# Own matmuls one step ahead, in the other half of the same PSUM banks, and a border that runs over 64 steps

## The chip, the cores and the metric

The kernel runs on one core of a Trainium2 chip. The metric is the time of one execution in microseconds of device time. The engines are named as in the profile: PE is TensorE's matmul stream and PEld its weight loads, DVE is VectorE, ACT is ScalarE, POOL is GpSimd, and SP issues most of the DMAs.

## The reference

The input `x` is 4 images of 64 channels, 256 x 256, in fp32. Two layers follow, each a group norm, a mixing step and a residual sum. Layer 0 is not touched by the change. Layer 1 is a GRU that runs over the columns of the image:

```python
def step(prev_col, cur_col):
    nb = jnp.concatenate([pad, prev_col, pad], axis=1)
    x = jnp.concatenate([nb[:, :-2], nb[:, 1:-1], nb[:, 2:]], axis=-1)
    new = _gru_cell(x.reshape(B * H, 3 * Cf), cur_col.reshape(B * H, Cf), ...)
    ...
# the cell: gi = x @ w_ih.T + b_ih, gh = h @ w_hh.T + b_hh, then
r = sigmoid(i_r + h_r);  z = sigmoid(i_z + h_z);  n = tanh(i_n + r * h_n)
return (1.0 - z) * n + z * h
```

The roles are unusual. The "input" of the cell is the result of the column before, at the rows h-1, h and h+1 (three taps). Its "hidden state" is the normalized column itself. So the products with `w_hh` depend on the input alone and can be made at any time, while those with `w_ih` need the column just finished. There are 255 steps, one after another.

## The kernel before

**Layout of layer 1.** A column of all four images is a tile of 128 partitions (two images x 64 channels) x 2 slots x 256 rows. Every product is done as four 64 x 64 quarters of TensorE's array (`quarters`, line 810): the row half of the array picks one of the two slots of a PSUM tile, the column half one of the two halves of the partitions. A PSUM tile of a gate is `[P, 2, 512]` in fp32, so it has two banks, one for each slot. Four such tiles, `hr`, `hn`, `hz` and `ni`, fill all eight banks. Before the change only 256 of the 512 columns of a bank are used.

**A step** (`column`, line 822) makes for column w:

- own matmuls of three gates (line 826): r into `pshr`, n into `pshn`, z into `pshz`, each of four quarters with 256 rows and the weights `wh`, from the normalized column `xn` and a copy `xt` with swapped halves;
- taps: three gates of three taps, of four quarters each, with the weights `wi` from the state `st` of the column before. The taps of r and z add to the own matmuls in `pshr` and `pshz`; those of n go to `psni` by themselves.

The rows are cut in two parts, [0, at) and [at, 256). `parts` (line 799) moves the border up by one row in each step, so that part 0 of a step, which needs one row more to each side, reads part 0 of the step before alone. After `SKEW` steps the border jumps back; a step where it has jumped is called a wrap (`wraps`, line 849), and there part 0 needs both parts of the step before. With `SKEW = 32` part 0 has 144 rows at a wrap and 113 at the end, part 1 has 112 to 143.

**The order on TensorE** is the program's order; a wrapper keeps every engine's instructions in it. In a usual step it is: own r; taps r of part 0; own n; own z; taps n and z of part 0; taps r, n and z of part 1. At a wrap the three own groups come first. The profile counts each fp32 matmul as two instructions, so four quarters are 8 and a group of taps is 24.

**Behind the taps** `state` (line 864) does, for each part: on ACT `g` = sigmoid of `pshr`, a normalize for a later column (`xn<-raw`), `z` = sigmoid of `pshz`, then tanh; on DVE a scalar_tensor_tensor from `pshn` and `g` (`n<-pshn,bias_sb,g`), the sum with `psni`, a scalar_tensor_tensor `g<-z,xn`, a product `n<-n,z` and the difference that writes the state `st`. POOL copies `xt`, adds the state to the raw column and clears the edges of the state tiles.

Waits between engines are put in by the framework that builds the program, tile by tile, from what each instruction reads and writes.

Of the kernel before, what the change touches and what calls it, by code (L numbers as in the profile page):

```python
# [9 lines left out]
F32 = mybir.dt.float32  # L10
# [5 lines left out]
B, C, W, H = 4, 64, 256, 256  # L16
HID = 6 * C
E = 2 * C
P = 128
# [143 lines left out]
def tile_conv_then_gru(  # L163
# [47 lines left out]
    with tc.tile_pool(name="xa", bufs=5) as xa, tc.tile_pool(name="sta", bufs=1) as sta, tc.tile_pool(  # L211
        name="bps", bufs=1, space=PSUM
# [9 lines left out]
        banks = bps.tile([P, 8, 512], F32, tag="b", name="psb")  # L222
# [7 lines left out]
        for i in range(32):  # L230
            kind, s = i // 16, i % 16
            c0, num = 2 * P * kind, 2 * P - P * kind
            ps = banks[0:HALO, 4 * (i % 2) : 4 * (i % 2) + 4, 0:num]
            for k in range(4):
# [6 lines left out]
                    stop=True,  # L241
# [34 lines left out]
    with layer0 as s:  # L276
# [19 lines left out]
        def normalize(n, jq):  # L296

            t, b, at = xq[n, jq], n // 8, n % 8
            flat = t.rearrange("p j k -> p (j k)")
            shift, rstd = sc0[:, b, 0:1], sc0[:, b, 1:2]  # L300
            if jq == 3:
                nc.vector.tensor_scalar(flat, flat, rstd, shift, ALU.mult, ALU.add)
            else:
                nc.scalar.activation(flat, flat, AF.Identity, bias=shift, scale=rstd)
            grid = t.rearrange("p j (r c) -> p j r c", c=10)
            if jq % 2 == 0:
                nc.gpsimd.memset(grid[:, 0, :, 0:1], 0.0)
            else:
                nc.gpsimd.memset(grid[:, 15, :, 9:10], 0.0)
            if at == 0 and jq < 2:  # L310
                nc.gpsimd.memset(grid[0:C, :, 0, :], 0.0)
            if at == 7 and jq >= 2:
                nc.gpsimd.memset(grid[C:P, :, 9, :], 0.0)
# [427 lines left out]
    WB = 8  # L741
    with ExitStack() as s:
# [3 lines left out]
        ps_g = s.enter_context(tc.tile_pool(name="ps_g", bufs=1, space=PSUM))  # L746
        raws, xns, xts, stcols = {}, {}, {}, {}
# [11 lines left out]
        def load_column(w):  # L759
            raws[w] = rawp.tile([P, 2, H], F32, tag="raw", name=f"raw_{w}")  # L760
            for of, to in column_parts(x1, w):
                nc.sync.dma_start(to, of)
# [5 lines left out]
        def empty_states(n):  # L768
            stcols[n] = st = colp.tile([P, 2, WB, H + 2], F32, tag="st", name=f"st_{n}")
            nc.gpsimd.memset(st[:, :, :, 0:1], 0.0)  # L770
            nc.gpsimd.memset(st[:, :, :, H + 1 : H + 2], 0.0)
# [19 lines left out]
        def add(w):  # L791
            nc.gpsimd.tensor_tensor(raws[w], raws[w], stcols[w // WB][:, :, w % WB, 1 : H + 1], ALU.add)
            for to, of in column_parts(out, w):
                nc.sync.dma_start(to, of)

        QUARTERS = ((0, 0), (0, 1), (1, 0), (1, 1))
        SKEW = 32

        def parts(w):


            at = H // 2 + SKEW // 2 - (w - 1) % SKEW
            return (0, at), (at, H)

        MAX = H // 2 + SKEW // 2

        def bank_pair(gate, w):
            return ps_g.tile([P, 2, 512], F32, tag=gate, name=f"ps{gate}_{w}")

        def quarters(ps, weights, rhs, start, stop, skip=False):  # L810
            for r, c in QUARTERS:
                nc.tensor.matmul(
                    ps[c * C : (c + 1) * C, r],
                    lhsT=weights[r * C : (r + 1) * C],
                    rhs=rhs(r, c),
                    start=start,
                    stop=stop,
                    tile_position=(r * C, c * C),
                    skip_group_check=skip,
                )  # L820

        def column(w):

            i, xn, xt, st = w % WB, xns[w // WB], xts[w // WB], stcols[(w - 1) // WB]

            def own(gate, bank, stop):

                ps = bank_pair(bank, w)[:, :, 0:H]
                quarters(
                    ps,  # L830
                    wh[:, gate, :],
                    lambda r, c: (xn[:, c] if r == c else xt)[r * C : (r + 1) * C, i, :],
                    True,
                    stop,
                )
                return ps

            def taps(ps, gate, h0, h1, start, skip=False):
                for t in range(3):
                    quarters(  # L840
                        ps,
                        wi[:, 3 * gate + t, :],
                        lambda r, c: st[r * C : (r + 1) * C, c, (w - 1) % WB, h0 + t : h1 + t],
                        start and t == 0,
                        t == 2,
                        skip,
                    )

            wraps = (w - 1) % SKEW == 0
            pr = own(0, "hr", False)  # L850
            pn = own(2, "hn", True) if wraps else None
            pz = own(1, "hz", False) if wraps else None
            for part in range(2):
                h0, h1 = parts(w)[part]
                pi = bank_pair("ni", f"{w}_{part}")[:, :, 0 : h1 - h0]
                taps(pr[:, :, h0:h1], 0, h0, h1, False, part == 1)
                if pz is None:
                    pn = own(2, "hn", True)
                    pz = own(1, "hz", False)
                taps(pi, 2, h0, h1, True)  # L860
                taps(pz[:, :, h0:h1], 1, h0, h1, False, part == 1)
                state(w, part, pn[:, :, h0:h1], pr[:, :, h0:h1], pi, pz[:, :, h0:h1])

        def state(w, part, pn, pr, pi, pz):
            h0, h1 = parts(w)[part]
            i, num = w % WB, h1 - h0
            xn, st = xns[w // WB], stcols[w // WB]
            g = gk.tile([P, 2, MAX], F32, tag=f"g{part}", name=f"g_{w}_{part}")[:, :, 0:num]
            n = gk.tile([P, 2, MAX], F32, tag=f"n{part}", name=f"n_{w}_{part}")[:, :, 0:num]
            z = gk.tile([P, 2, MAX], F32, tag=f"z{part}", name=f"z_{w}_{part}")[:, :, 0:num]  # L870
            nc.scalar.activation(g, pr, AF.Sigmoid, bias=b_rz[:, 0:1], scale=1.0)
            for more in range(ahead(w - 1), ahead(w)):
                normalize(more, part)
            nc.vector.scalar_tensor_tensor(n, pn, bias_sb[:, 5:6], g, ALU.add, ALU.mult)
            nc.vector.tensor_tensor(n, pi, n, ALU.add)

            nc.scalar.activation(z, pz, AF.Sigmoid, bias=b_rz[:, 1:2], scale=-1.0)
            nc.scalar.activation(n, n, AF.Tanh, bias=bias_sb[:, 2:3], scale=1.0)
            nc.vector.scalar_tensor_tensor(g, z, -1.0, xn[:, :, i, h0:h1], ALU.add, ALU.mult)
            nc.vector.tensor_tensor(n, n, z, ALU.mult)  # L880
            nc.vector.tensor_tensor(st[:, :, i, 1 + h0 : 1 + h1], n, g, ALU.subtract)

        def ahead(w):

            return min(2 * w + 4, w + WB + 1, W)
# [5 lines left out]
                normalize(w, slot)  # L891
        empty_states(0)
        nc.vector.tensor_copy(stcols[0][:, :, 0, 1 : H + 1], xns[0][:, :, 0])
        for w in range(W):
            if w % WB == 0 and w + WB < W:
                empty_states(w // WB + 1)
            if w:
                column(w)
            add(w)
            if w + 2 * WB < W:  # L900
                load_column(w + 2 * WB)
# [60 lines left out]
```

## Time and profile before

| | |
|---|---|
| runs of the kernel before | 5144.2, 5144.63, 5165.15 us; median 5144.63 us |
| the profiled execution | 5172.3 us, its span 5170.4 us |
| layer 0 and what lies between, by the first own matmul of layer 1 | the first 3806 us of the span |
| layer 1, first own matmul to last tap | 1356.5 us for 255 steps |
| most usual step of layer 1 | 5.23 us |
| granted TensorE clock of the profiled execution | 0.988 |

The profile is one execution on the chip, taken by the hardware profiler. Its rows give the busy time of an engine, or groups of instructions, or single instructions in order of time. All of this kernel's instructions are recorded by one helper, so every row has the same line number, L157, and the names of the tiles tell the rows apart: `pshr<-xn,wh` is an own matmul of r, `pshr<-st,wi` a tap of r. Matmuls overlap, and a row of 24 taps starts before the ones ahead of it have ended; lengths of groups on TensorE are therefore taken from the start of one to the start of the next.

### The profile page before, as it was taken

How to read it: one execution, taken by the hardware profiler on the slowest of the kernel's cores; microseconds unless marked ns; L12 is line 12 of the kernel's file. 1: busy time of each engine (PE TensorE's matmuls, PEld its weight loads, DVE VectorE, ACT ScalarE, POOL GpSimd, SP SyncE). 2: the span in 40 equal slices, each digit the busy share in tenths (PEclk: the TensorE clock that was granted, in tenths of full speed). 3: DMA queues.
4: the chain of work that ended last, by engine and by line, in shares of the span. 5: the costliest groups of instructions: out<-in, count | busy, mean ns of one | idle time of the engine just before them, and what ended most of it. 6: DMA issues, size and time to landing. Idle time of an engine off the chain costs nothing.

```text
span 5170.4 us, 276110 instructions
## 1 busy us (share of the span) xinstructions
PE 4885.9 (94%) x127092; PEld 4252.5 (82%) x127092; DVE 4033.3 (78%) x7000; ACT 3323.6 (64%) x4253; POOL 1732.9 (34%) x1723
## 2 busy tenths in 40 slices
PE   3999999999999999999999999999969999999999
PEld 2878788888888788888787888888859999999998
DVE  4778788888788777887787878777867777777777
ACT  3666666666666566666566667666656666666665
POOL 0233333333333233333333324323243333333333
PEclk9999999999999999999999999999989999999999
DMA  7566676666667666566666656556543333333332
GB/s 257 152 163 174 166 187 174 174 164 171 170 176 185 166 169 173 167 173 174 169 180 173 168 140 162 152 160 169 147 111 105 104 102 103 103 106 102 104 102 73
DMA packets 421176, 784.57 MB, mean 152 GB/s; under 512 B 32604, under 2 KB 295552, under 8 KB 417632
## 3 DMA queue, kind: packets, MB, share of 16 engines
q1 hardware_dynamic: 366464, 533.76, 38.3%
q0 software_dynamic: 53264, 232.55, 15.4%
q8 instruction: 997, 16.33, 1.4%
q14 instruction: 163, 1.34, 0.1%
q10 hardware_dynamic: 288, 0.58, 0.1%
HBM read 622.72 MB, written 144.05 MB: 148 GB/s over the span
## 4 chain that ended last, share of the span: by engine, by line
PE 83%; issue 5%; ACT 4%; DMA 4%; DVE 3%; POOL 1%; ACTq 0%; POOLq 0%; SPq 0%; DVEq 0%
PE psring L157 58%; PE pshr L157 8%; PE pshz L157 8%; PE psni L157 6%; DMA t<-t_all 2%; PE pshn L157 2%; DVE wk L157 1%; ACT v L157 1%; ACT z L157 1%; ACT xq L157 1%; DVE z L157 1%; DVE bn L157 0%; DMA seen<-in_x 0%; DMA bt<-in_taps 0%; DMA wk<-in_sums 0%
## 5 line engine op out<-in xcount | busy, mean ns | idle before, releaser
L157 PEld LDWEIGHTS psring<-h,t 100*32 100x32 f32 x49152 | 1392.0, 120 | 252.0 <-issue 199.8
L157 PE MATMUL psring<-h,t 100*32 100x128 f32 x49152 | 1475.4, 258 | 97.7 <-issue 61.8
L157 PEld LDWEIGHTS psring<-w_sb,xq 64*100 64x100 f32 x24576 | 1371.8, 164 | 128.1 <-issue 93.7
L157 PE MATMUL psring<-w_sb,xq 64*100 64x128 f32 x24576 | 1429.9, 273 | 38.1 <-issue 24.1
L157 ACT COPY h<-psring 100x1024 f32<-100x1024 f32 (+2 forms) x1371 | 1235.2, 988 | 336.7 <-PE psring L157 335.5
L157 DVE TENSOR_TENSOR wk<-psring,wk 128x1024 f32<-128x1024 f32 (+1 forms) x768 | 759.2, 1036 | 469.3 <-PE psring L157 333.6
L157 POOL TENSOR_TENSOR v<-v,z 128x2048 f32<-128x2048 f32 x128 | 582.9, 4558 | 672.9 <-DVE wk L157 611.5
L157 DVE TENSOR_TENSOR z<-z,moments 128x2048 f32<-128x2048 f32 x256 | 577.9, 2278 | 2.3
L157 POOL TENSOR_TENSOR wk<-wk 128x1024 f32<-128x1024 f32 x128 | 303.4, 2370 | 614.0 <-DVE wk L157 561.9
L157 POOL TENSOR_TENSOR raw<-raw,st 128x512 f32<-128x512 f32 x256 | 303.6, 1186 | 539.0 <-DVE st L157 412.4
L157 ACT COPY z<-psring 128x2048 f32<-128x2048 f32 x128 | 239.0, 1867 | 351.1 <-PE psring L157 261.7
L157 ACT ACTIVATE z<-pshz,b_rz 128x288 f32<-128x288 f32 (+7 forms) x510 | 242.5, 476 | 338.5 <-PE pshz L157 333.0
L157 PE MATMUL pshr<-st,wi 64*64 64x144 f32 (+7 forms) x12240 | 450.7, 270 | 7.4 <-DVE st L157 6.6
L157 PE MATMUL psni<-st,wi 64*64 64x144 f32 (+7 forms) x12240 | 445.7, 269 | 0.2
L157 PE MATMUL pshz<-st,wi 64*64 64x144 f32 (+7 forms) x12240 | 445.5, 269 | 0.0
L157 DVE COPY h<-psring 100x1024 f32<-100x1024 f32 x229 | 276.9, 1211 | 208.8 <-PE psring L157 208.6
L157 PEld LDWEIGHTS pshr<-st,wi 64*64 64x64 f32 x12240 | 379.1, 133 | 50.2 <-DVE st L157 38.0
L157 ACT COPY wk<-psring 128x1024 f32<-128x1024 f32 x256 | 259.7, 1014 | 249.8 <-PE psring L157 221.0
L157 DVE BATCH_NORM_STATS2 lnst<-z 128x6 f32<-128x128 f32 x2048 | 416.7, 280 | 0.0
L157 ACT COPY v<-psring 128x2048 f32<-128x2048 f32 (+1 forms) x160 | 243.4, 1521 | 257.8 <-PE psring L157 257.5
L157 PEld LDWEIGHTS psni<-st,wi 64*64 64x64 f32 x12240 | 391.0, 133 | 21.5 <-issue 0.4
L157 PE MATMUL psring<-wk,g_sb 32*64 32x512 f32 x6144 | 383.0, 604 | 7.8 <-issue 3.8
(96 smaller groups left out, 6298.0 us busy)
## 6 DMA issues: line engine op xcount, KB each, us to landing
t<-t_all SPq DMA_DIRECT2D x768, 400.0 KB
xq<-in_xh POOLq DMA_DIRECT2D x128, 800.0 KB, 6.4
wk<-in_x SPq DMA_DIRECT2D x256, 256.0 KB
x<-wk POOLq DMA_DIRECT2D x256, 256.0 KB, 5.4
seen<-in_x POOLq DMA_DIRECT2D x96, 512.0 KB, 7.7
raw<-x SPq DMA_DIRECT2D x128, 256.0 KB
raw<-x SPq DMA_DIRECT2D x256, 128.0 KB
out<-raw SPq DMA_DIRECT2D x128, 256.0 KB
```

The source lines that it names most:

```text
L157: return self.tc.keep_in_program_order(got(*args, **kwargs))
```

## The change

`SKEW` goes from 32 to 64, so part 0 has 160 rows at a wrap and 97 at the end, and part 1 has 96 to 159. The four PSUM tiles are made once instead of once per use. Even and odd steps use columns 0 to 255 and 256 to 511 of the same banks, and for `ni` part 0 and part 1 do. The own matmuls of step w + 1 are all issued behind the last taps of step w, in the order r, n, z. At a wrap the own n of the step after it is issued ahead of the taps, and left out of the place behind them.

```diff
-        SKEW = 32
+        SKEW = 64
...
-        def bank_pair(gate, w):
-            return ps_g.tile([P, 2, 512], F32, tag=gate, name=f"ps{gate}_{w}")
+        banks = {g: ps_g.tile([P, 2, 512], F32, tag=g, name=f"ps{g}") for g in ("hr", "hn", "hz", "ni")}
+
+        def half_banks(gate, odd):
+            return banks[gate][:, :, 256 * odd : 256 * odd + 256]
...
-        def column(w):
-
-            i, xn, xt, st = w % WB, xns[w // WB], xts[w // WB], stcols[(w - 1) // WB]
-
-            def own(gate, bank, stop):
-
-                ps = bank_pair(bank, w)[:, :, 0:H]
+        owns = {}
+
+        def own(w, gates=(0, 2, 1)):
+            i, xn, xt = w % WB, xns[w // WB], xts[w // WB]
+            for gate in gates:
+                owns[w, gate] = half_banks(("hr", "hz", "hn")[gate], w % 2)
                 quarters(
-                    ps,
+                    owns[w, gate],
                     wh[:, gate, :],
                     lambda r, c: (xn[:, c] if r == c else xt)[r * C : (r + 1) * C, i, :],
                     True,
-                    stop,
+                    gate == 2,
                 )
-                return ps
+
+        def column(w):
+
+            st = stcols[(w - 1) // WB]
...
-            wraps = (w - 1) % SKEW == 0
-            pr = own(0, "hr", False)
-            pn = own(2, "hn", True) if wraps else None
-            pz = own(1, "hz", False) if wraps else None
+            if (w - 1) % SKEW == 0 and w + 1 < W:
+                own(w + 1, (2,))
+            pr, pz, pn = (owns.pop((w, gate)) for gate in range(3))
             for part in range(2):
                 h0, h1 = parts(w)[part]
-                pi = bank_pair("ni", f"{w}_{part}")[:, :, 0 : h1 - h0]
+                pi = half_banks("ni", part)[:, :, 0 : h1 - h0]
                 taps(pr[:, :, h0:h1], 0, h0, h1, False, part == 1)
-                if pz is None:
-                    pn = own(2, "hn", True)
-                    pz = own(1, "hz", False)
                 taps(pi, 2, h0, h1, True)
                 taps(pz[:, :, h0:h1], 1, h0, h1, False, part == 1)
                 state(w, part, pn[:, :, h0:h1], pr[:, :, h0:h1], pi, pz[:, :, h0:h1])
+            if w + 1 < W:
+                own(w + 1, (0, 1) if (w + 1, 2) in owns else (0, 2, 1))
...
         nc.vector.tensor_copy(stcols[0][:, :, 0, 1 : H + 1], xns[0][:, :, 0])
+        own(1)
         for w in range(W):
```

## The prediction

> **What bounds the kernel now.** I read the page first, then the windows by stage, the list of waits inside layer 1, and last the timeline of single steps. The page says which engine fills the span:
>
> ```profile
> PE 4885.9 (94%) x127092; PEld 4252.5 (82%) x127092; DVE 4033.3 (78%) x7000; ACT 3323.6 (64%) x4253; POOL 1732.9 (34%) x1723
> ```
>
> That is a mean over both layers. The windows (length, busy time of PE, PEld, DVE, ACT and POOL, granted clock, DMA share, GB/s) show the middle of layer 1:
>
> ```profile
> 4000.00:4500.00 500.00, 497.04 (x15828) 468.05 (x15824) 390.38 (x942) 335.54 (x755) 191.77 (x307) 1.00 0.36 103
> ```
>
> TensorE is idle for 3 us in 500, at full clock. From one first own matmul to the next I read a step as 5.23 us in most of the 255 cases, the same for any border: an own group takes 0.432 us, a group of taps 0.0155 us + 0.005 us a row (0.725 for 142 rows, 0.586 for 114), so 3 x 0.432 + 6 x 0.0155 + 3 x 256 x 0.005 = 5.23. 255 such steps are 1334 us, and the layer takes 1356.5. No order of the same matmuls can win more than those 23 us, 0.45%. The waits inside the layer (us in total, times, longest) say where some of it lies:
>
> ```profile
> PEld pshr L157 <- DVE st L157: 38.0, 108, 1.5
> PE pshr L157 <- DVE st L157: 6.6, 7, 1.0
> ...
> PEld pshz L157 <- ACT z L157: 1.5, 6, 0.3
> PEld pshn L157 <- DVE n L157: 1.4, 6, 0.4
> ```
>
> The first two are taps that wait for the state, mostly covered by matmuls still running. The last two are small, but are what the change multiplies: an own n that waits for VectorE's read of `pshn`, an own z that waits for ACT's read of `pshz`. Before, that can show only at wraps, where own n and z stand straight behind own r. The timeline at a wrap, behind a part 1 of 143 rows:
>
> ```profile
> 4488.14 0.51 DVE L157 SCALAR_TENSOR_TENSOR n<-pshn,bias_sb,g 128x286 f32<-128x286 f32 x1
> 4488.34 0.38 PE L157 MATMUL pshr<-xn,wh 64*64 64x256 f32 x1
> ...
> 4488.77 0.38 PE L157 MATMUL pshn<-xn,wh 64*64 64x256 f32 x1
> ...
> 4490.36 0.46 DVE L157 TENSOR_TENSOR st<-n,g 128x286 f32<-128x286 f32 x1
> 4490.87 0.97 PE L157 MATMUL pshr<-st,wi 64*64 64x144 f32 x24 [0.89 <-DVE st L157]
> ```
>
> The read of `pshn` ends at 4488.65, before own n is due at 4488.77: no wait. The taps then wait 0.89 us for part 1 of the state and start 0.05 after it ends. The next step, part 1 of 112 rows:
>
> ```profile
> 4494.85 0.38 PE L157 MATMUL pshr<-xn,wh 64*64 64x256 f32 x1
> ...
> 4494.88 0.46 DVE L157 TENSOR_TENSOR st<-n,g 128x288 f32<-128x288 f32 x1
> ...
> 4495.16 0.45 ACT L157 ACTIVATE z<-pshz,b_rz 128x224 f32<-128x224 f32 x1
> ...
> 4495.26 0.44 DVE L157 SCALAR_TENSOR_TENSOR n<-pshn,bias_sb,g 128x224 f32<-128x224 f32 x1
> 4495.40 0.96 PE L157 MATMUL pshr<-st,wi 64*64 64x143 f32 x24
> ...
> 4496.18 0.38 PE L157 MATMUL pshn<-xn,wh 64*64 64x256 f32 x1
> ```
>
> Now the read of `pshn` ends at 4495.70, 0.85 us after own r starts. Before it costs nothing, since the taps of r stand between. Behind own r, own n would be due at 4495.28.
>
> **What is added: own n waits for the same bank.** The halves would remove the wait if waits went by columns. The built order of the changed kernel says they don't. Followed to the instruction that each count belongs to, own n of step w + 1 waits for VectorE's `n<-pshn,bias_sb,g` of step w, part 1; own z for ACT's z of step w, part 1; own r for ACT's g. All three read the other half of the bank. Taps n of part 1 still wait for the sum with `psni` of part 0, so the halves of `ni` free nothing.
>
> The trace can't show whether columns apart matter, as before reuses the same ones. The Trainium skill, "PSUM — Partial Sum Buffer", section "PSUM bank collisions raise a hardware error", gives the rule that speaks against this change: guard PSUM by bank and quadrant, not by address, because two engines in one bank collide at any column. Guarded by address the sum would be about -12 us (the removed part below, without the own z term), by bank it is the one below.
>
> So each own n starts at the later of T + 0.432 (T is the start of own r) and the end of VectorE's read + 0.055, the release measured where taps wait for the state. I read that end over all steps, as medians by the rows of part 1: 0.849 us behind T at 112, 0.726 at 118, 0.606 over 127 to 129, 0.41 to 0.50 at 136 to 140, 0.320 at 143. It falls because part 1's taps cover the chain that precedes the read: z of part 0 on ACT, tanh, product, state, then this read; VectorE keeps its order, so the read stands behind part 0's state. By blocks of a new cycle of 64 steps, the wait being lag + 0.055 - 0.432:
>
> - 96 to 111 rows: not in the trace. The slope from 112 to 118, 0.0205 a row, carries on (a row less takes 0.015 of cover and lengthens four operations): mean lag 1.023, wait 0.646, x 16 = 10.3 us. If the lag stayed flat at 0.849 it would be 7.6.
> - 112 to 127: mean lag 0.728, wait 0.351, x 16 = 5.6.
> - 128 to 143: what is over zero sums to 1.9.
> - 144 to 159: none.
>
> Own z is due at T + 0.863; ACT's z of part 1 ends 0.75 (112 rows) to 0.864 (143) behind T. Only where own n does not wait does it show: 0.03 rising to 0.11, 1.35 us over the last 20 steps. A cycle costs 17.9 + 1.35 = 19.2, and 255 steps are four cycles: **+77 us**. What queues behind own n is all of TensorE; own n and own z hold back every tap of the next step.
>
> **What is removed.** Taps r of part 0 wait after each border jump: steps 1 to 7 of a cycle are longer by 0.165, 0.14, 0.12, 0.09, 0.075, 0.05, 0.03, together 0.67, x 8 = 5.4 us. After the change own n's wait ends later than that state does, so this goes whole. Wraps: 7 steps of 6.47 instead of 5.23, 8.7 us. After it 3 remain; with four own groups ahead (1.73 us) and part 1's state about 2.5 behind T, each waits some 0.75, 2.3 us. On the step after a wrap own n is done early, and own z waits 0.38 in place of own n's 0.8: -1.6 over four. Together -5.4 - 8.7 + 2.3 - 1.6 = **-13.4**.
>
> **Edits with no price.** The wider border leaves TensorE's sum of taps at 5.23 (rows sum to 256). Own matmuls one step early need `xn` and `xt` of w + 1, at the same place of the stream as own r before. SP's and POOL's queues are not reordered. Own n of step 2 ahead of the first taps moves 0.9 us of work, not adds it. Taps n and z of part 0 follow r at once now, so `g` and the sum with `psni` have 1.31 us less 0.3 of cover, and needed 1.8 behind taps r against a tanh that waits for z anyway until 2.1: 0.3 spare.
>
> **Sum.** 77 - 13.4 = +64 us. The profiled execution would go from 5172.3 to about 5236; it stands 27.7 above the median, and I carry the difference over: 5144.63 + 64 = 5209. Bounds of the main term: a flat lag under 112 rows takes off 4 x 2.7 = 11, and the lower ones of the scattered lags 5 to 8 more; the upper ones, 0.1 us on some 40 waiting steps, add 17. So +45 to +81, 5190 to 5226.
>
> A second page speaks of such idle time. "TensorE: Matmul & The Clock Gate", "A second HAM failure mode: psum-queue depth-cycling", tells of frequent small idles that make the clock fall. The trace has gaps of 0.89 us at clock 1.00, and I set nothing; by the page, half clock in the 45 or so waiting steps of a cycle would be, as an estimate from their 5.2 us, 900 us.
>
> **Rivals.**
>
> - *The halves work, no own group waits.* Then only the removed part counts: -5.4 - 8.7 + 2.3 = -12 us, 5133, not slower (within 0.5%). It decides if own n starts 0.432 behind own r at 96 rows. For it: nothing else in the trace holds TensorE. Against: the waits in the built order. 5%.
> - *The spare 0.3 us above is not there*, since VectorE is 78% busy, and its sum with `psni` comes late in every step. Then late steps wait too, by about 0.2 us: 255 x 0.2 = 51 more, 5260. For it: VectorE's chain already ends close to TensorE's turn. Against: it ends part 1's state 2.5 us behind T, before taps r of part 0 are read. 10%.
> - *The lags shrink*, because part 0's own chain starts at the same time but with nothing of the step before left on VectorE: below half of the term, about 5165 or less. 3%.
>
> **How the numbers follow.** My forecast has 82%: 5209, range 5190 to 5226. For 8 in 10 I widen for the second rival and for the spread of the runs before (5165.15 lies 20 above their median): 5186 to 5240. About 0.5%, 26 us, is what a measurement of this kernel can tell from no change. Faster by more needs over 23 us won, the whole idle time: 1%. Same: the first and third rivals, 7%. Slower: 92%.
>
> **What would show it.** Right: in the waits of layer 1, `pshn` on DVE n rises from 1.4 us and 6 times to the largest wait of TensorE, some 60 to 80 us over 160 to 180 steps; steps start a cycle near 6.0 us, fall by 0.02 each, and reach 5.25 to 5.30 from about 140 rows; waits of `pshr` taps on DVE st all but vanish outside 3 wraps. Wrong: own n starts 0.43 behind own r at 96 rows; steps at 150 rows over 5.35; or a granted clock under 0.95 in this layer.

## The result and the profile after

| | before | after |
|---|---|---|
| median of six runs each | 5145.49 us (5133.86 to 5165.15) | 5200.45 us (5196.04 to 5208.04) |
| ratio, after to before | | 1.0108, 95% interval 1.0089 to 1.0128, so 46 to 66 us |
| profiled execution, span | 5172.3, 5170.4 us | 5200.1, 5198.2 us |
| first own matmul of layer 1 | 3806.0 us into the span | 3768.5 us |
| layer 1, first own matmul to last tap | 1356.5 us | 1421.9 us, +65.3 |

The change is slower by 55 us, where 64 was forecast. The two profiled executions differ by 28 us only: the one before reached layer 1 some 37 us later, over code that the change does not touch. So layer 1 is compared by itself, in all that follows.

The page after has the same engine on top, busy for 25 us more with the same number of instructions:

```profile
PE 4910.6 (94%) x127092; PEld 4200.5 (81%) x127092; DVE 4053.6 (78%) x7000; ACT 3343.7 (64%) x4253; POOL 1732.8 (33%) x1723
```

In the windows (columns as before) TensorE's idle time in 500 us of layer 1 has grown from 3 us to 10 and 16, at an unchanged clock of 1.00:

```profile
4000.00:4500.00 500.00, 490.06 (x15230) 430.54 (x15223) 385.89 (x907) 330.30 (x725) 185.56 (x297) 1.00 0.35 99
4500.00:5000.00 500.00, 484.08 (x14941) 422.61 (x14934) 374.13 (x889) 322.94 (x711) 179.45 (x289) 1.00 0.34 98
```

The busy time hides part of the loss, since ends of matmuls are modelled. The waits of layer 1 after the change (us, times, longest) name it:

```profile
PEld pshn L157 <- DVE n L157: 106.1, 195, 0.9
...
PE pshn L157 <- DVE n L157: 27.7, 85, 0.5
PEld pshz L157 <- ACT z L157: 24.7, 89, 0.6
...
PEld pshr L157 <- DVE st L157: 3.0, 3, 1.0
...
PE pshr L157 <- DVE st L157: 1.7, 3, 0.6
```

Own n waiting for VectorE has gone from 1.4 us and 6 times to the largest wait of TensorE. Taps waiting for the state have gone from 108 times to the 3 wraps. A weight load's wait (PEld) overlaps the matmuls still running, and a row of PE counts only from the modelled end of the matmuls before it; the time lost to own n lies between the two. A step early in a cycle, behind a part 1 of 97 rows:

```profile
4139.99 0.43 PE L157 MATMUL pshr<-xn,wh 64*64 64x256 f32 x1
...
4140.18 0.49 DVE L157 TENSOR_TENSOR st<-n,g 128x318 f32<-128x318 f32 x1
...
4140.59 0.42 DVE L157 SCALAR_TENSOR_TENSOR n<-pshn,bias_sb,g 128x194 f32<-128x194 f32 x1
4141.06 0.43 PE L157 MATMUL pshn<-xn,wh 64*64 64x256 f32 x1 [0.40 <-DVE n L157]
...
4141.54 0.38 PE L157 MATMUL pshz<-xn,wh 64*64 64x256 f32 x1
```

VectorE reads the other half of the bank until 4141.01, and own n starts 0.05 later, 1.07 us behind own r instead of 0.43. Late in a cycle, behind 150 rows, the same read is over in time and own n starts 0.44 behind own r:

```profile
4791.26 0.52 DVE L157 SCALAR_TENSOR_TENSOR n<-pshn,bias_sb,g 128x300 f32<-128x300 f32 x1
...
4791.62 0.38 PE L157 MATMUL pshr<-xn,wh 64*64 64x256 f32 x1
...
4792.06 0.38 PE L157 MATMUL pshn<-xn,wh 64*64 64x256 f32 x1
...
4792.98 0.72 PE L157 MATMUL pshr<-st,wi 64*64 64x105 f32 x24
...
4793.48 0.47 DVE L157 TENSOR_TENSOR st<-n,g 128x300 f32<-128x300 f32 x1
```

The last two rows show that waits are finer in SBUF: the taps of r read part 0's rows of the state while VectorE is yet to write part 1's rows of the same tile, and do not wait for that.

From one own r to the next, steps start a cycle at 6.03 us, fall by 0.02 each to 5.27 at the 42nd, and lie from the 48th on at 5.27 to 5.31 but for single longer ones, where before they were 5.40 falling to 5.23.

### The profile page after: what moved, and what is told of

Same layout as the page of the kernel before. It is cut to its first block, busy times and chain, and to the rows that moved or that the text cites. A ratio compares the mean times of both kernels' runs of the same rounds, so it can differ in the third digit from the quotient of the medians.

```text
span 5198.2 us, 275867 instructions
## 1 busy us (share of the span) xinstructions
PE 4910.6 (94%) x127092; PEld 4200.5 (81%) x127092; DVE 4053.6 (78%) x7000; ACT 3343.7 (64%) x4253; POOL 1732.8 (33%) x1723
## 4 chain that ended last, share of the span: by engine, by line
PE 78%; DVE 7%; issue 5%; ACT 5%; DMA 3%; POOL 1%; ACTq 0%; SPq 0%; POOLq 0%; DVEq 0%
PE psring L157 57%; PE pshz L157 7%; PE pshr L157 6%; PE psni L157 5%; PE pshn L157 3%; DMA t<-t_all 2%; ACT z L157 2%; DVE n L157 2%; DVE wk L157 1%; ACT v L157 1%; DVE st L157 1%; DVE g L157 1%; ACT xq L157 1%; DVE z L157 1%; DMA wk<-in_sums 1%
## 5 line engine op out<-in xcount | busy, mean ns | idle before, releaser
L157 PE MATMUL pshr<-st,wi 64*64 64x160 f32 (+15 forms) x12240 | 429.7, 269 | 1.7 <-DVE st L157 1.7
L157 PE MATMUL pshz<-st,wi 64*64 64x160 f32 (+15 forms) x12240 | 429.7, 269 | 0.9 <-issue 0.6
L157 PE MATMUL psni<-st,wi 64*64 64x160 f32 (+15 forms) x12240 | 428.7, 269 | 0.6 <-issue 0.5
L157 ACT ACTIVATE g<-pshr,b_rz 128x320 f32<-128x320 f32 (+15 forms) x510 | 240.3, 471 | 222.7 <-PE pshr L157 222.7
L157 PEld LDWEIGHTS pshz<-st,wi 64*64 64x64 f32 x12240 | 359.0, 133 | 2.4 <-issue 2.0
```

Source lines behind the costliest of these rows:

```text
L157: return self.tc.keep_in_program_order(got(*args, **kwargs))
```

## The experiments

All compare the length of layer 1 in the profile, one profiled execution for each kernel; ratios of whole runs stand beside it. "Wait" means time from the start of a group on TensorE to the next, less the group's own 0.432 us.

### The border back to 32 steps, the rest as changed

```diff
-        SKEW = 64
+        SKEW = 32
```

> The changed kernel with the border over 32 steps again, all else as changed. Layer 1, first own matmul to last tap, was 1356.5 us before and 1421.9 us after the change in the profiles. Theory (own n waits for VectorE's read of the other half of its bank): part 1 has 112 to 143 rows, where the wait is 0.53 falling to 0, about 7.5 us in each of 8 cycles, 60 us, less some 9 us for taps that no longer wait: layer 1 at 1400 to 1410 us, 45 to 53 us over before. Rival (the wide border is the price, the own matmuls and halves cost nothing): layer 1 at 1345 us, no slower than before.

Layer 1 took 1406.5 us, +50.0 over before; the ratio to before is 1.0098 (1.0080 to 1.0115). Own n waits 45.6 us in 189 steps. So most of the price is there with the old border.

### The border over 64 steps, the rest as before

```diff
-        SKEW = 32
+        SKEW = 64
```

> The kernel before with the border over 64 steps, all else as before. Theory: own n stays behind the taps of r, so it does not wait; the taps of r of part 0 wait for the state where part 1 has 96 to 119 rows, up to 0.5 us a step, and 3 wraps are left instead of 7: layer 1 about 15 us over before, 1366 to 1378 us. Rival (the border is the price): most of the 65 us, 1410 to 1422 us.

1369.0 us, +12.4; ratio 1.0042 (1.0021 to 1.0063). What waits is the taps of r, for the state (before: 38.0 us, 108 times, and 6.6 us, 7 times):

```profile
PEld pshr L157 <- DVE st L157: 50.2, 119, 1.4
PE pshr L157 <- DVE st L157: 3.0, 3, 1.0
```

The wider border is a loss by itself: fewer wraps save less than a small part 1 costs. From start to start the taps of r lose 23.0 us, against 12.8 before, and own r, which waits for ACT's `g`, 3.5 against 0.3.

The two prices, 50.0 and 12.4, add up to 62.4 of the 65.3 us, but not because the same waits add. In the changed kernel the taps of r wait at the 3 wraps alone. There the wider border costs 15.4 us (1421.9 less 1406.5) by another way, mostly own n, which waits 57.9 us instead of 45.6.

### No halves

```diff
         def half_banks(gate, odd):
+            odd = 0
...
-            if (w - 1) % SKEW == 0 and w + 1 < W:
-                own(w + 1, (2,))
```

> The changed kernel with columns 0 to 255 of every bank used by every step and both parts, so no halves; the own n group of the step after a wrap goes back behind the last taps, since its bank is still to be read at a wrap. Theory (waits go by bank, so the halves free nothing): the waits are the same, layer 1 at 1421 to 1427 us against 1421.9 with halves; the early own n at four wraps is worth 2 us. Rival (the halves free part of the waits, as of own z or of the taps n): layer 1 over 1440 us.

1423.8 us against 1421.9; ratio to before 1.0130 (1.0112 to 1.0149). Own n waits 61.9 us in 162 steps, as against 57.9 in 156 with halves. The 2 us are what the early own n was expected to be worth. The halves free nothing that TensorE waits for.

### Even and odd steps in different banks

```diff
-        banks = {g: ps_g.tile([P, 2, 512], F32, tag=g, name=f"ps{g}") for g in ("hr", "hn", "hz", "ni")}
+        pairs = [ps_g.tile([P, 2, 512], F32, tag=f"rn{k}", name=f"psrn{k}") for k in range(2)]
+        banks = {g: ps_g.tile([P, 2, 512], F32, tag=g, name=f"ps{g}") for g in ("hz", "ni")}
         def half_banks(gate, odd):
+            if gate in ("hr", "hn"):
+                at = 256 * (gate == "hn")
+                return pairs[odd][:, :, at : at + 256]
...
-        def own(w, gates=(0, 2, 1)):
+        def own(w, gates=(2, 0, 1)):
...
-                own(w + 1, (0, 1) if (w + 1, 2) in owns else (0, 2, 1))
+                own(w + 1, (0, 1) if (w + 1, 2) in owns else (2, 0, 1))
```

> The changed kernel with the same PSUM cut another way: hr and hn of even steps share one pair of banks, hr and hn of odd steps another pair, so even and odd steps use different banks for r and n; the order of the own groups is n, r, z. Theory (waits go by bank): own n and own r wait for nothing, own z hardly; new is that taps r of part 1 share a bank with VectorE's read of n of part 0 and wait up to 0.1 us a step for it, 16 us in all: layer 1 at 1362 to 1376 us, 46 to 60 us under the changed kernel. Rival (own matmuls behind the last taps are dear for another reason, such as the normalized columns or the array): layer 1 stays at 1415 to 1425 us.

1371.5 us, 50 under the changed kernel; ratio to before 1.0049 (1.0032 to 1.0067). The same own matmuls stand at the same place and use the same bytes of PSUM, and 50 of the 65 us are gone. The waits of own z, whose halves are as they were, and of r and n, now both in `psrn`:

```profile
PEld pshz L157 <- ACT z L157: 68.0, 248, 0.8
...
PEld psrn L157 <- DVE n L157: 5.5, 32, 0.2
PEld psrn L157 <- DVE st L157: 3.0, 3, 1.0
...
PE psrn L157 <- DVE st L157: 1.7, 3, 0.6
```

The 106 us and 195 times of `pshn` on DVE n have become 5.5 and 32. The largest wait left is own z's for ACT's read of the other half. Most of its 68 us is covered by matmuls still running: from start to start own z loses 7.3 us, against 0.8 before. The taps in part 1 lose 10.5 (r) and 7.6 us (n), against 0.5 and 1.2 before, and own n and the taps of r in part 0 lose less than before. The expectation had put all of the 15 us over before on the taps of r in part 1, and own z at hardly anything.

### VectorE does not read own n

```diff
-            nc.vector.scalar_tensor_tensor(n, pn, bias_sb[:, 5:6], g, ALU.add, ALU.mult)
+            nc.vector.scalar_tensor_tensor(n, xn[:, :, i, h0:h1], bias_sb[:, 5:6], g, ALU.add, ALU.mult)
```

> The changed kernel in which VectorE's first operation of a part reads the normalized column from SBUF in place of the own n product from PSUM; so the result leaves the own n product out, the matmuls are all made. Theory: own n has no reader to wait for, the term of 59 us measured between own r and own n goes, own r and own z keep their small waits: layer 1 at 1355 to 1368 us. Rival (own n is late for another reason): layer 1 at 1415 to 1425 us.

A miss: 1423.5 us; ratio 1.0200 (1.0158 to 1.0242). The profile is of the fastest of four executions, 5201.9 us where the median was 5234.7. The wait between own r and own n did go, from 57.9 us to 1.4, but another took its place, taps n for VectorE's sum of the part before:

```profile
PEld psni L157 <- DVE n L157: 58.7, 76, 1.0
PE psni L157 <- DVE n L157: 39.3, 73, 0.8
```

The operation put in its place did not cost the same. These are the groups of the two operations, of this kernel and then of the changed one (count, busy us, mean ns):

```profile
L157 DVE SCALAR_TENSOR_TENSOR n<-xn,bias_sb,g 128x312 f32<-128x312 f32 (+15 forms) x480 | 318.8, 664 | 24.9 <-ACT g L157 21.7
```

```profile
L157 DVE SCALAR_TENSOR_TENSOR n<-pshn,bias_sb,g 128x200 f32<-128x200 f32 (+15 forms) x478 | 230.1, 481 | 110.6 <-ACT g L157 110.0
```

With both inputs in SBUF it took 664 ns in the mean instead of 481, and up to 1627. Steps fall into two kinds, 5.23 to 5.4 us and 5.9 to 6.3, in runs of many. So the run shows that the reader is what own n waits for, and nothing of what the layer costs without the wait.

When the operation is slow can be read from the same trace: when POOL works beside it, its sum `raw<-raw,st` above all. Here are two of the same shape, the first with the sum beside it, the second with POOL idle:

```profile
3830.07 1.28 POOL L157 TENSOR_TENSOR raw<-raw,st 128x512 f32<-128x512 f32 x1 [2.16 <-DVE st L157]
3830.09 1.59 DVE L157 SCALAR_TENSOR_TENSOR n<-xn,bias_sb,g 128x302 f32<-128x302 f32 x1 [0.15 <-ACT g L157]
...
4440.02 0.53 DVE L157 SCALAR_TENSOR_TENSOR n<-xn,bias_sb,g 128x302 f32<-128x302 f32 x1
```

The 18 operations with no POOL work beside them took 518 ns in the mean, and the 18 such ones that read `pshn` in the changed kernel 517. The 52 that ran over 1 us beside POOL's sum took 1402 ns, and the 222 beside its copies alone 583, where 221 that read `pshn` took 474. The operation that reads `pshn` was not slowed: at 128x302 it took 527 ns alone and 531 beside the sum. POOL's sum was slower too, 1290 ns in the mean instead of 1188.

### Own z ahead of own n

```diff
-                own(w + 1, (0, 1) if (w + 1, 2) in owns else (0, 2, 1))
+                own(w + 1, (0, 1) if (w + 1, 2) in owns else (0, 1, 2))
```

> The changed kernel with the own groups behind the last taps in the order r, z, n instead of r, n, z. Theory: own z then is due 0.43 us behind own r, while ACT's read of the other half ends 0.75 to 0.83 behind it whatever the rows of part 1, so it waits 0.37 to 0.46 in every step, also in late ones; own n behind it waits for nothing: 252 steps x 0.415 = 105 us in place of 69 for own n and own z, layer 1 at 1450 to 1468 us. Rival (no wait by bank, or own n alone is held): layer 1 at or under 1422 us.

1461.4 us, in a kernel that was run once (5266.3 us). Own z waits 104.6 us, in 253 of 253 steps, the 105 expected. One of them:

```profile
4303.13 0.38 PE L157 MATMUL pshr<-xn,wh 64*64 64x256 f32 x1
...
4303.44 0.46 ACT L157 ACTIVATE z<-pshz,b_rz 128x238 f32<-128x238 f32 x1
...
4303.95 0.43 PE L157 MATMUL pshz<-xn,wh 64*64 64x256 f32 x1 [0.21 <-ACT z L157]
```

ACT's read of the other half of `pshz` ends at 4303.90, own z starts 0.05 later. The row's 0.21 counts from the modelled end of own r; from own r's start it is 0.82, so 0.39 over its due time. The wait does not go by columns for ACT either.

### A version meant to beat both

It takes the pairs of banks from above and moves the own groups to where they cover something:

```diff
-                own(w + 1, (2,))
...
+            if wraps:
+                if w + 1 < W:
+                    own(w + 1, (2, 0))
+                own(w, (1,))
...
                 taps(pi, 2, h0, h1, True)
+                if not part and not wraps:
+                    own(w, (1,))
                 taps(pz[:, :, h0:h1], 1, h0, h1, False, part == 1)
                 state(w, part, pn[:, :, h0:h1], pr[:, :, h0:h1], pi, pz[:, :, h0:h1])
+                if not part and not wraps and w + 1 < W:
+                    own(w + 1, (2, 0))
-            if w + 1 < W:
-                own(w + 1, (0, 1) if (w + 1, 2) in owns else (0, 2, 1))
```

With `SKEW = 64`:

> A version meant to beat both: hr and hn of even and odd steps in different pairs of banks; own n and r of the next step stand between the taps of part 0 and part 1, where they wait for nothing and cover part 0's chain; own z stands ahead of the taps z of part 0; the border over 64 steps. Theory: no own group waits, taps r of part 0 only in the first steps of a cycle, and three wraps are left at about 1.1 us: layer 1 at 1340 to 1356 us against 1356.5 before, 0 to 16 us faster than before. Rival (VectorE's chain, at 4.4 us of a 5.2 us step, becomes the bound once nothing else waits): layer 1 over 1370 us.

With `SKEW = 48`:

> The same version with the border over 48 steps, so part 1 has 104 to 151 rows: five wraps at 1.1 us instead of three, and less waiting of taps r where part 1 is small. Theory: within 4 us of the version with 64 steps, layer 1 at 1340 to 1356 us. Rival (narrow parts are what costs in the version with 64 steps): 5 us or more under it.

Layer 1 took 1357.4 and 1354.6 us; the ratios to before are 0.9996 (0.9980 to 1.0011) and 0.9995 (0.9979 to 1.0010). So neither beats the kernel before: the first lies just over its expected range, the second near the upper edge of its own. The long waits for the state are down to the border jumps (of the version with 48 steps):

```profile
PEld psrn L157 <- DVE st L157: 10.6, 10, 1.4
...
PE psrn L157 <- DVE st L157: 7.3, 10, 0.9
```

From start to start TensorE loses 23.9 us with 64 steps and 21.0 with 48, where it lost 23.0 before. A border jump costs twice, some 1.2 us on its own step and 0.7 to 0.9 on the next, where 1.1 was expected; the rest is many small waits. VectorE was slower as well, busy 416 us in 500 instead of 390: `g<-z,xn` took 512 ns in the mean against 459 before, the product `n<-n,z` 485 against 433. In the version with 48 steps 156 of 496 operations `g<-z,xn` ran over 0.05 us beside POOL's sum (8 of 495 before); these took 642 ns, the others 450. What the slower VectorE cost TensorE is not shown. There were only some 20 us to win.

## Why the prediction was right

**The main step held: own n waits for VectorE's read of the other half.** 156 of 245 usual steps wait, 57.9 us in all, against 71 forecast for own n, or 68 without the four early ones that the removed part takes out again. The sign named was 60 to 80 us over 160 to 180 steps in the list of waits; the rows there are 106.1 us over 195 and 27.7 over 85, and the loss from start to start lies just under it. That the columns do not matter is settled by three runs: no halves cost the same, other banks take 50 us off, and the other order moves the wait to own z. Whether the waits go by bank or by the whole PSUM tile no run separates, since every PSUM tile here fills whole banks; in SBUF, as the rows above show, they do not go by the whole tile.

**The sizes, by the prediction's blocks**, for a cycle of 64 steps. Own n's wait was 8.7 us at 96 to 111 rows (10.3 forecast, 9.5 without the early own n at 96 rows), 5.1 at 112 to 127 (5.6), 0.9 at 128 to 143 (1.9), none above (none). Two things make up for it, and the prediction had given a price to neither. At 96 to 105 rows own r itself is late, held by ACT's `g`: 3.3 us over the four cycles, so the lag from own r, 1.015 at 96, came out below the extrapolated 1.18, and the sum of both waits near it. And a group that starts after an idle takes 0.48 us instead of 0.432, its first matmuls 0.43 instead of 0.38: 0.05 x 156 = 8 us. Own z over the last 20 steps of a cycle cost some 5 us in all, against 5.4, but not as forecast: it starts only 0.01 to 0.02 late, where 0.03 to 0.11 was forecast, and most of the rest is again the 0.05 us of a group after an idle.

**The removed part held.** Taps r of part 0 wait no more outside the wraps. A wrap waits 0.79 us (0.75 forecast), and on the step after it own z waits 0.37 (0.38).

**Together** +65.3 us of layer 1 in the profiles, +64 forecast. Sorted by the group that starts late, with the prediction's own lengths of groups, TensorE lost 23.0 us before and 88.3 after: own n +54.0, own z +11.8, own r +4.7, taps of r -6.1, all others +1.0 (the 0.05 us of a group after an idle counts with the group behind it). That the sum came within 2 us is in part luck: own n's wait came out smaller than forecast, and what had no price made up for it. The median of the runs moved by 55, inside its interval of 46 to 66. It can't be held to 10 us when the same layer 0 ends up to 37 us apart from one profiled execution to the next.

**The rivals.** That the halves work is refuted by the runs without them. That VectorE lacks the spare 0.3 us did not show: taps n of part 1 wait 1.3 us in all. It is a near thing all the same, as the run with the slower operation shows: there taps n wait 59 us in the list of waits. That the lags shrink is refuted by the lags, 0.852 us at 112 rows as before.

**The clock.** Idles of up to 0.69 us in most steps left it at 1.00 in the windows above. The case told in "TensorE: Matmul & The Clock Gate" of the Trainium skill, of a clock that falls with frequent small idles, is not this one. The rule of "PSUM — Partial Sum Buffer", section "PSUM bank collisions raise a hardware error", keeps the work of two engines apart by bank, and the waits in this kernel agree with it: own n starts 1.07 us behind own r, behind a reader of other columns. The runs show such waits; what happens without them was not tried.

## What to carry to other kernels

Two halves of a PSUM bank are not two buffers: where waits go by bank, the next step's matmul still waits for the reader of the other half, and a second buffer has to be another bank, if need be by pairing different tensors in one; here that took back 50 of 65 us. Before work is moved ahead, look for the last reader of what it overwrites, and price the move by how late that reader ends behind the new place; here the kernel before had that figure in its own timeline. And count first what there is to win: 3 idle us in 500 leave nothing that would pay for a new wait.

## What was not expected

A group of matmuls that starts after an idle of TensorE takes 0.05 us more than one in a stream, at full clock. A VectorE operation with both inputs in SBUF took up to 1.6 us beside a sum of POOL and 518 ns without, while the same operation with one input in PSUM was not slowed; the slowness came in long runs of steps that stayed slow. Identical code of layer 0 brought the first own matmul of layer 1 at 3768.5 to 3806.0 us into the span.
